# A two-layer decoder in one kernel: five small moves in the order of work

## The chip, the cores and the metric

The kernel runs on one core of a Trainium2 chip as a single launch. The metric is the device time of an execution in microseconds (us). Three runs of the kernel before give 2009.89, 2010.07 and 2011.51 us, so its time is 2010.07 us, the median. One more execution was recorded by the hardware profiler; it took 2007.35 us, and all rows below are from it.

The engines are TensorE (PE in the profile; its weight loads are PEld), VectorE (DVE), ScalarE (ACT), GpSimd (POOL) and SyncE (SP). In this kernel SP issues all plain DMAs, and POOL issues the indirect ones. Each engine carries out its instructions in order, and a DMA that has to wait on SP holds up whatever stands behind it on SP.

## What is computed

The reference is a decoder with two layers over 8 sequences of 112 tokens (896 tokens of width 512, float32), with a context of 8 x 375 rows. Each of the six parts reads a layer norm of the running sum and is added to it:

```python
x = x + L0_attn(layernorm(x), ...)                    # causal attention, 16 heads
x = x + L0_xattn(layernorm(x), ctx_2048, mask, ...)   # attention to the context
x = x + L0_ffn(layernorm(x), ...)                     # attention, then 32 experts, 8 a token
x = x + L1_attn(layernorm(x), ...)                    # causal attention, 32 heads, a bias
x = x + L1_xattn(layernorm(x), ctx_2048, mask, ...)   # attention to the context, gated
x = x + L1_ffn(layernorm(x), ...)                     # silu(x @ wg) * (x @ wu) @ wd
```

The masks of the two cross-attentions mark context rows that count or don't. For the inputs at hand only the last 96 rows of a context (`TAIL`) differ from their neighbours in the mask; all rows before (`EARLY`, 279) are masked. The kernel counts on the chip whether this holds, and has a general path if it doesn't.

## The kernel before

The tokens are seven tiles of 128 rows, `x[0]` to `x[6]`, held in SBUF; `hT` is the normalised and transposed copy (feature on the partitions) that matmuls read. The parts run one after the other, but a scheduler lays each engine's instructions out ahead of time, and it lets work of one part run beside the end of the one before where its data and memory allow it. Inside `with in_order():` the instructions of DVE, ACT, POOL and PE keep the order of the source (`Engine.issue_next`); DMAs are not pinned by it.

**Memory and waits.** A `phase` opens two pools of SBUF tiles. With `waits="pool"` the first use of a new tile waits until the whole of an older pool on the same addresses is done with; with `"tile"` it waits only for the old tiles under it. `normed_rows()` hands out a ring of three row tiles `xn`; each use waits until the third use before it is over, its store to DRAM among it. `load_w` takes one of six buffers of 1 MB (`wp`) in the same way.

**Mask counts.** `any_early()` loads both masks, counts on DVE, POOL and PE the early rows that are not masked, and leaves two numbers, `early0` and `early1`. It is called ahead of `l0_self_attention()`. Each cross-attention reads its number into a register of every engine (`by_early`) and branches to `from_last_keys` (the path taken here) or `from_all_keys`.

**First cross-attention** (`l0_cross_attention`). Its `from_last_keys` runs over the 8 sequences: scores, exponentials, the values of the sequence (`values(b)`), the turn of the outputs of the sequence before the last, the averages of the last one, and, from b = 3 on, output products and the next norm for the first `LATE` = 4 tiles (`go_on`). Behind the loop come the last turn, the last average, the end of the fourth tile and one more turn.

**Keys and values for the second cross-attention.** They depend on the context alone, so they are made earlier and kept in DRAM: `last_keys` makes the keys (`far_keys`), `last_values(b, cT, wv)` the values of one sequence (`far_values`): four matmuls, a copy by ACT into a row of the `xn` ring, and a store issued by SP. The values are made at the start of the experts (`l0_block_experts`): five sequences in the loop that normalises and transposes the tiles for the router, three in the stage that works out which token goes to which expert (`names_of`), as filling for PE. Their contexts are loaded into `wbuf[3]`, a buffer for expert weights that is not yet in use. The keys are made behind the last expert block.

**End of the experts.** The experts add their results into two DRAM arrays, `accs[0]` and `accs[1]`. Behind `last_keys` the seven `x[t]` are loaded from the first, then seven `odd[:, t]` from the second, and DVE adds them. The next layer's norms and projections follow.

**Second cross-attention and last feed-forward.** `l1_cross_attention` has a pinned loop over b = 0 to 8; in it the output products of the tiles 0 to 4 update `x[t]`; tiles 5 and 6 follow behind the branch. Then `l1_feed_forward` normalises all seven tiles (`layernorm_T`: statistics on DVE, square root on ACT, reciprocal and scaling on DVE, transposes on PE, a copy by ACT). Its matmuls use a scheme with seven products for eight, which needs sums of the two token halves of `hT` (`column_sums`, DVE, `tok`) and sums of weight blocks (`row_sums`, POOL, `sums`). `rsqrt_newton` gives the same root as `rsqrt`, by 14 small operations on POOL instead of ACT.

Most of the loops record their instructions under one line of the source, L80 (a pinned instruction), so the rows of the profile are told apart by the names of their tiles.

## Time and profile before

| what | us |
|---|---|
| median of three runs | 2010.07 |
| profiled execution, whole | 2007.35 |
| its span, first to last instruction | 2005.6 |
| PE / DVE / POOL / ACT busy | 1893.5 / 965.0 / 907.9 / 689.6 |
| mean granted TensorE clock (1 is full) | 0.975 |
| first attention | 0 to 160 |
| first cross-attention, its loop | 160 to 324, 212 to 311 |
| attention of the first layer's block | 324 to 872 |
| router and naming | 872 to 964 |
| expert blocks | 964 to 1350 |
| keys for the second cross-attention, reload of the tiles | 1350 to 1377 |
| second attention | 1377 to 1610 |
| second cross-attention | 1610 to 1741 |
| last feed-forward | 1741 to 2005 |

Times of stages are places in the profiled span. A row of the timeline gives start, length, engine, line, operation, output and input tiles with shapes, and a count where equal instructions are merged; in brackets stands how long the engine was idle before it and what ended the wait. The table of stages gives, for stretches of the span, the busy time of each engine, the granted clock, the share of the 16 DMA engines in use and the rate. The profile's digits per fortieth of the span are tenths.

### The profile page before, as it was taken

The page shows a single profiled execution, that of the slowest core. Times are in us where ns is not written, and L with a number is a line of the kernel's source. Part 1 is how long each engine was busy: PE and PEld are TensorE (multiplying, and loading weights), DVE is VectorE, ACT ScalarE, POOL GpSimd, SP SyncE. Part 2 cuts the span into 40 slices and gives each one's busy share as a digit, 9 for nine tenths or more (in the row PEclk, how much of TensorE's full clock was granted, in tenths as well). Part 3 has the DMA queues.
Part 4 walks back from the last instruction along what each step waited for, and adds up shares of the span by engine and source line. Part 5 has one row for each costly group of instructions (what it writes and reads, how often), then busy time and mean ns, then how long its engine had stood idle before and what let it go on. Part 6 is the DMA issues. An engine that isn't in the chain of part 4 may idle for free. (4 is left out here: it accounts for less than half of the span.)

```text
span 2005.6 us, 28210 instructions
## 1 busy us (share of the span) xinstructions
PE 1893.5 (94%) x10345; PEld 1233.2 (61%) x10345; DVE 965.0 (48%) x1993; ACT 689.6 (34%) x1941; POOL 907.9 (45%) x1099
## 2 busy tenths in 40 slices
PE   8999999999999999989999999998888798799999
PEld 4555565456666666754778888874456554455568
DVE  4562466486676676525222222214579656612160
ACT  3543321044444444532111111112368645432200
POOL 2253042256766765631466666640355312344371
PEclk9999988999999999989999999999999899999999
DMA  4105010233444444644986777754000020211100
GB/s 180 43 22 165 24 58 28 72 129 138 163 138 161 142 147 152 209 155 163 307 251 126 191 176 168 190 82 158 1 23 2 33 72 11 86 42 42 42 8 29
DMA packets 87469, 217.05 MB, mean 108 GB/s; under 512 B 33427, under 2 KB 41363, under 8 KB 78228
## 3 DMA queue, kind: packets, MB, share of 16 engines
q1 hardware_dynamic: 63028, 141.61, 21.0%
q0 software_dynamic: 24288, 73.47, 14.3%
q8 instruction: 87, 1.43, 0.3%
q14 instruction: 66, 0.54, 0.1%
HBM read 248.98 MB, written 82.43 MB: 165 GB/s over the span
## 5 line engine op out<-in xcount | busy, mean ns | idle before, releaser
L80 PEld LDWEIGHTS bank<-hbT,wb 128*128 128x128 f32 x1408 | 164.5, 192 | 20.5 <-issue 20.1
L80 DVE TENSOR_TENSOR hidb<-sgb,bank 128x256 f32<-128x256 f32 x66 | 27.8, 421 | 287.0 <-ACT sgb L80 213.8
L80 PE MATMUL bank<-hbT,wb 128*128 128x128 f32 x1408 | 165.0, 276 | 0.0
L1089 ACT ACTIVATE s<-s,mn 112x112 f32<-112x112 f32 x256 | 97.5, 382 | 125.1 <-DVE mn L1083 114.4
L80 POOL TENSOR_TENSOR st<-st,rec 112x448 f32<-112x448 f32 (+1 forms) x95 | 82.8, 903 | 123.4 <-DVE rec L80 77.4
L932 POOL TENSOR_TENSOR qT<-qT,qs 128x448 f32<-128x448 f32 x64 | 77.7, 1214 | 108.0 <-DVE qs L928 108.0
L80 POOL DMA_INDIRECT acc<-ob,row_out x66 | 106.3, 1610 | 35.0 <-issue 18.3
L80 ACT ACTIVATE st<-st,mxs 112x112 f32<-112x112 f32 (+1 forms) x383 | 110.9, 377 | 0.0
L80 ACT ACTIVATE sgb<-bank 128x256 f32<-128x256 f32 x66 | 25.3, 383 | 204.9 <-PE bank L80 169.6
L80 POOL DMA_INDIRECT hrow<-hrows,row_in x66 | 63.7, 965 | 54.9 <-DMA a_wo<-in_a_wo 27.3
L1096 POOL TENSOR_TENSOR s<-s,rec 112x448 f32<-112x448 f32 x64 | 64.2, 1004 | 50.2 <-DVE rec L1095 47.5
L80 POOL DMA_INDIRECT wb<-weights,wrow x44 | 46.3, 1053 | 80.8 <-PE bank L80 63.4
L80 PE MATMUL bank<-wb,hidb 128*128 128x512 f32 x176 | 82.8, 593 | 0.0
L80 ACT ACTIVATE ob<-bank,pw 128x512 f32<-128x512 f32 x66 | 45.4, 688 | 108.8 <-PE bank L80 108.8
L843 PE MATMUL bank<-tok,sums 128*128 128x448 f32 x192 | 78.1, 541 | 1.9 <-DVE tok L827 1.4
L843 PE MATMUL bank<-osum,osums 128*128 128x256 f32 x288 | 74.9, 386 | 1.4 <-POOL osums L820 1.0
L1072 PEld LDWEIGHTS bank<-kT,qT 128*112 128x112 f32 x512 | 61.6, 178 | 21.5 <-DVE s L1078 9.2
L80 PE MATMUL bank<-ident,st 112*112 112x112 f32 (+1 forms) x384 | 52.4, 271 | 21.5 <-POOL st L80 16.8
L1072 PE MATMUL bank<-kT,qT 128*112 128x112 f32 x512 | 63.1, 263 | 6.1 <-DVE s L1078 6.1
L1047 POOL TENSOR_TENSOR y<-y,oc 128x256 f32<-128x256 f32 x63 | 51.2, 817 | 38.7 <-DVE y L1045 28.7
L843 PEld LDWEIGHTS bank<-osum,osums 128*128 128x128 f32 x288 | 53.1, 192 | 24.3 <-issue 14.6
L928 DVE TENSOR_TENSOR qs<-xn,shape_consts 64x448 f32<-64x448 f32 x84 | 66.9, 797 | 1.5
(450 smaller groups left out, 4352.1 us busy)
## 6 DMA issues: line engine op xcount, KB each, us to landing
weights<-in_e_wg SPq DMA_DIRECT2D x64, 256.0 KB
weights<-in_e_wu SPq DMA_DIRECT2D x64, 256.0 KB
weights<-in_e_wd SPq DMA_DIRECT2D x64, 256.0 KB
f_wq<-in_f_wq SPq DMA_DIRECT2D x8, 1024.0 KB
f_wo<-in_f_wo SPq DMA_DIRECT2D x8, 1024.0 KB
cTe<-in_ctxT SPq DMA_DIRECT2D x8, 558.0 KB
f_wg<-in_f_wg SPq DMA_DIRECT2D x4, 1024.0 KB
f_wu<-in_f_wu SPq DMA_DIRECT2D x4, 1024.0 KB
```

Source lines behind the costliest of these rows:

```text
L80: done = issue(*args, **kw)
L843: T.matmul(dst, lhs(k), rhs(k), start=first and k == 0, stop=k == terms - 1, skip_group_check=True)
L928: V.tensor_tensor(qs[lo : lo + 64], src[hi : hi + 64], sin0[lo : lo + 64].unsqueeze(1).to_broadcast([64, HB, S]), ALU.mult,)
L932: G.tensor_tensor(d, d, qs, ALU.add)
L1047: G.tensor_tensor(d, d, more, ALU.add)
L1072: T.matmul(bank[5][:S, j * S : (j + 1) * S], qT[:, j, tok], keys[hg // 2 % 2][:, tok], start=True, stop=True)
L1089: A.activation(s[:, j, :], s[:, j, :], AF.Exp, bias=mn[:, j : j + 1], scale=-1.0, accum_out=den[:, j : j + 1])
L1096: G.tensor_tensor(s, s, rec.unsqueeze(2).to_broadcast([S, 4, S]), ALU.mult)
```

## The change

It has five parts. (1) `any_early()` is called behind `l0_self_attention()` instead of ahead of it. (2) The reload of the token tiles goes in pairs: `x[t]`, then `odd[:, t]`. (3) The values of the sequences 0 to 4 (`FAR` = 5) for the second cross-attention are made in the first: three in the rounds b = 5, 6, 7 of its loop, two behind the last average; their contexts are already there (`cTt`), and the weights `c1_wv` are loaded once more, as a fifth matrix at the start of that part. At the experts' start the sequences 5 to 7 are made in the loop over tiles, and none in the naming stage. (4) The stores of `last_keys` and `last_values` are issued by ACT. (5) The last norm goes in steps: in the second cross-attention, one round behind the update of a tile, `find_scale` works out its scale (with the root on POOL), and another round later the first three tiles are scaled into the rows of the `xn` ring; the last feed-forward takes these and does the rest of the norm for the other four. Its phase and its two inner pools wait by tile instead of by pool. The functions `last_contexts`, `last_keys` and `last_values` move up in the source.

```diff
     def last_keys(contexts, wk_):
...
-                nc.sync.dma_start(far_keys[:, c, bs, :].rearrange("p b k -> p (b k)"),
-                                  kT[:, : HB * TAIL])
+                nc.scalar.dma_start(far_keys[:, c, bs, :].rearrange("p b k -> p (b k)"),
+                                    kT[:, : HB * TAIL])
     def last_values(b, cT, wv):
...
-        nc.sync.dma_start(far_values[:, b, :], va[:TAIL])
+        nc.scalar.dma_start(far_values[:, b, :], va[:TAIL])
...
     def l0_cross_attention(early, y):
-        wq, wk_, wv, wo = (load_w(a[n], n) for n in ("c0_wq", "c0_wk", "c0_wv", "c0_wo"))
+        wq, wk_, wv, wo, c1_wv = (
+            load_w(a[n], n) for n in ("c0_wq", "c0_wk", "c0_wv", "c0_wo", "c1_wv")
+        )
...
+            def values_of_next(b):
+                return last_values(b, cTt[:, b, :, :TAIL], c1_wv)
...
                         go_on(b - 3)
+                        if b >= B - 3:
+                            all_of(values_of_next(b - B + 3))
                         waiting = b, va
                     turn_outputs(oT, *turning, tp_ps())
                     turning = average(*waiting)
+                    for b in range(3, FAR):
+                        all_of(values_of_next(b))
                     go_on(LATE - 1)
...
             for t, _ in enumerate(rmsnorm_rows_T(hT, hrows, y, ln2w)):
-                if t < 5:
-                    all_of(values_of_next(t))
+                if t < B - FAR:
+                    all_of(values_of_next(FAR + t))
...
-                far = [values_of_next(b) for b in range(5, B)]
-                next(far[0])
                 names_of(0, 2)
-                all_of(far[0])
...
                 for t in range(4, NTT):
-                    if t < 6:
-                        next(far[t - 3])
                     shared_out(t - 4)
                     names_of(t, 0)
-                    if t < 6:
-                        all_of(far[t - 3])
...
+            odd = yp.tile([P, NTT, D], FP, tag="y", name="odd")
             for t in range(NTT):
                 nc.sync.dma_start(x[t], accs[0][t * P : (t + 1) * P, :])
-            odd = yp.tile([P, NTT, D], FP, tag="y", name="odd")
-            for t in range(NTT):
                 nc.sync.dma_start(odd[:, t, :], accs[1][t * P : (t + 1) * P, :])
                 V.tensor_tensor(x[t], x[t], odd[:, t, :], ALU.add)
...
+            scales = [sm.tile([P, 4], FP, tag="mvr", name="mvr", bufs=8) for _ in range(LATE)]
+            rows = [normed_rows() for _ in range(3)]
+
+            def find_scale(t):
+                st = sm.tile([P, 6], FP, tag="bn", name="bn")
+                V.bn_stats(st, x[t])
+                V.bn_aggr(scales[t][:, :2], st)
+                rsqrt_newton(scales[t][:, 2:3], scales[t][:, 1:2], ONCE)
...
                         if b < B:
                             divide(b)
+                        if 0 <= b - 5 < len(rows):
+                            normed(rows[b - 5], x[b - 5], scales[b - 5])
+                        if 0 <= b - 4 < LATE:
+                            find_scale(b - 4)
...
-        with phase("f1") as p0:
+        with phase("f1", "tile") as p0:
             hT = new_hT()
-            layernorm_T(hT)
+            for t in range(NTT):
+                if t < len(rows):
+                    xn = rows[t]
+                else:
+                    mvr = scales[t] if t < len(scales) else row_scales(x[t])
+                    xn = normed_rows()
+                    normed(xn, x[t], mvr)
+                transpose_tile(hT, xn, t)
...
-                gp = pools.enter_context(tc.tile_pool(name="gates", bufs=1))
+                gp = pools.enter_context(tc.tile_pool(name="gates", bufs=1, reuse_waits="tile"))
...
-            with tc.tile_pool(name="down", bufs=1) as dp:
+            with tc.tile_pool(name="down", bufs=1, reuse_waits="tile") as dp:
...
-    early0, early1 = any_early()
     l0_self_attention()
+    early0, early1 = any_early()
...
-    l1_cross_attention(early1, l1_self_attention())
-    l1_feed_forward()
+    l1_feed_forward(*l1_cross_attention(early1, l1_self_attention()))
```

More of the change, by code (lines that the diff above doesn't have):

```diff
@@ L569, in tail_keys, with last_contexts, last_keys, last_values @@
                     A.activation(kT[:, c, bs, :], src, AF.Identity, bias=bias[:, c : c + 1])
+    far_keys = tc.dram_tile([P, KC, B, TAIL], FP, name="far_keys")
+    far_values = tc.dram_tile([TAIL, B, D], FP, name="far_values")
+    FAR = 5
+    def last_contexts(pool, half):
+        cT = pool.tile([P, HB, KC, TAIL], FP, tag=f"cTk{half}", name=f"cTk{half}")
+        for i in range(HB):
+            nc.sync.dma_start(cT[:, i], a["ctxT"][half * HB + i][:, :, EARLY:])
+        return cT
+    def last_keys(contexts, wk_):
+        for half, cT in enumerate(contexts):
+            bs = slice(half * HB, (half + 1) * HB)
+            for c in range(KC):
+                pp = mm_ps()
+                matmul_k(pp[:, : HB * TAIL], lambda k: wk_[:, k, c * P : (c + 1) * P],
+                         lambda k: cT[:, :, k, :])
+                kT = normed_rows()
+                A.copy(kT[:, : HB * TAIL], pp[:, : HB * TAIL])
+                nc.scalar.dma_start(far_keys[:, c, bs, :].rearrange("p b k -> p (b k)"),
+                                    kT[:, : HB * TAIL])
+    def last_values(b, cT, wv):
+        pp = tp_ps()
+        matmul_k(pp[:TAIL, :], lambda k: cT[:, k, :], lambda k: wv[:, k, :])
+        yield
+        va = normed_rows()
+        A.copy(va[:TAIL], pp[:TAIL, :])
+        nc.scalar.dma_start(far_values[:, b, :], va[:TAIL])
+        yield
     def l0_cross_attention(early, y):
-        wq, wk_, wv, wo = (load_w(a[n], n) for n in ("c0_wq", "c0_wk", "c0_wv", "c0_wo"))
+        wq, wk_, wv, wo, c1_wv = (
+            load_w(a[n], n) for n in ("c0_wq", "c0_wk", "c0_wv", "c0_wo", "c1_wv")
+        )
         with phase("c0") as p0:
@@ L762, in from_all_keys @@
                         pass
+                for b in range(FAR):
+                    all_of(values_of_next(b))
             by_early(early, "c0", from_last_keys, from_all_keys)
@@ L781, in by_early @@
         work[0] = outer
-    far_keys = tc.dram_tile([P, KC, B, TAIL], FP, name="far_keys")
-    far_values = tc.dram_tile([TAIL, B, D], FP, name="far_values")
-    def last_contexts(pool, half):
-        cT = pool.tile([P, HB, KC, TAIL], FP, tag=f"cTk{half}", name=f"cTk{half}")
-        for i in range(HB):
-            nc.sync.dma_start(cT[:, i], a["ctxT"][half * HB + i][:, :, EARLY:])
-        return cT
-    def last_keys(contexts, wk_):
-        for half, cT in enumerate(contexts):
-            bs = slice(half * HB, (half + 1) * HB)
-            for c in range(KC):
-                pp = mm_ps()
-                matmul_k(pp[:, : HB * TAIL], lambda k: wk_[:, k, c * P : (c + 1) * P],
-                         lambda k: cT[:, :, k, :])
-                kT = normed_rows()
-                A.copy(kT[:, : HB * TAIL], pp[:, : HB * TAIL])
-                nc.sync.dma_start(far_keys[:, c, bs, :].rearrange("p b k -> p (b k)"),
-                                  kT[:, : HB * TAIL])
-    def last_values(b, cT, wv):
-        pp = tp_ps()
-        matmul_k(pp[:TAIL, :], lambda k: cT[:, k, :], lambda k: wv[:, k, :])
-        yield
-        va = normed_rows()
-        A.copy(va[:TAIL], pp[:TAIL, :])
-        nc.sync.dma_start(far_values[:, b, :], va[:TAIL])
-        yield
     def row_sums(dst, top, bottom, eng):
@@ L2132, in from_all_keys @@
                     all_of(project_out(t))
+                    find_scale(t)
+                    if t < len(rows):
+                        normed(rows[t], x[t], scales[t])
             by_early(early, "c1", from_last_keys, from_all_keys)
@@ L2136, in l1_cross_attention, with l1_feed_forward @@
                 all_of(project_out(t))
-    def l1_feed_forward():
-        with phase("f1") as p0:
+        return rows, scales
+    def l1_feed_forward(rows, scales):
+        with phase("f1", "tile") as p0:
             hT = new_hT()
-            layernorm_T(hT)
+            for t in range(NTT):
+                if t < len(rows):
+                    xn = rows[t]
[4 more added lines that the diff above has]
+                transpose_tile(hT, xn, t)
             h = p0.tile([P, 16, NT], FP, tag="hid", name="hid")
             with ExitStack() as pools:
-                gp = pools.enter_context(tc.tile_pool(name="gates", bufs=1))
+                gp = pools.enter_context(tc.tile_pool(name="gates", bufs=1, reuse_waits="tile"))
                 tokens = [gp.tile([P, 2, HALF], FP, tag=f"tok{i}", name=f"tok{i}") for i in range(4)]
@@ L2244, in l1_feed_forward @@
                 in_turn(two_tiles(p) for p in range(NTT // 2))
+    l0_self_attention()
     early0, early1 = any_early()
-    l0_self_attention()
     with tc.tile_pool(name="y", bufs=1) as yp:
```

## The prediction

> **What bounds the kernel.** I read the busy shares first, then the chain of waits, then the timeline and the table of stages at the four places that the diff touches.
>
> ```profile
> span 2005.6 us, 28210 instructions
> ...
> PE 1893.5 (94%) x10345; PEld 1233.2 (61%) x10345; DVE 965.0 (48%) x1993; ACT 689.6 (34%) x1941; POOL 907.9 (45%) x1099
> ...
> PE   8999999999999999989999999998888798799999
> ```
>
> TensorE is busy 94% of the span and no other engine over half, so time can only come out of PE's gaps, or out of PE work that moves into a gap. The digits below 9 are at the start, at slice 18 (start of the experts) and in slices 27 to 34 (end of the experts to the last feed-forward). Every edit but one lies at such a place; the exception, the end of the first cross-attention, reads as a 9, so work put there has to be paid.
>
> The profiled execution took 2007.35 us: the span and 1.75 around it. The three runs have a median of 2010.07, 2.72 more. I sum against the profiled execution and take the same difference off the median.
>
> **Stores on ACT's queue, tiles reloaded in pairs (end of the experts).** The timeline there (start, length, engine, line, what; in brackets the idle time before and what ended it):
>
> ```profile
> 1358.39 0.38 SPq L803 DMA_DIRECT2D far_keys<-xn  x1
> ...
> 1363.72 0.48 ACT L80 COPY xn<-bank 128x384 f32<-128x384 f32 x1 [4.96 <-DMA far_keys<-xn]
> ...
> 1366.12 0.69 DVE L1674 TENSOR_TENSOR x<-x,odd 128x512 f32<-128x512 f32 x1 [20.49 <-DMA odd<-acc]
> ...
> 1369.58 7.12 PE L80 MATMUL bank<-cTk,c_wk 128*128 128x384 f32 x16 [2.47 <-ACT xn L80]
> ```
>
> The eight key products are 64 matmul records of 0.32 us: started at 1350.27 they could end at 1371.0; they end at 1376.7. The reader sees why: their results go through a ring of three xn rows, and the stores that free the ring stand in SP's order among 14 tile loads. The first result is ready at 1353.6, and its store is issued at 1358.39. PE loses 0.84 and 2.47 us idle and some 2 us to the lower clock that follows (0.78 in 1371 to 1377). From the last key product to the first projected chunk (1376.53 to 1390.05) PE is nearly full, so what the keys end earlier, the next layer starts earlier, if its inputs are there. With x[0], odd[0], x[1], odd[1] in turn the fourth tile is loaded after 8 transfers, not 11; I put its sum at 1367 to 1369 against 1370.3. That is in time only for an end of the keys at 1371; the score biases, now issued before 1366, should land by 1372. Next late: the bias rows and the third xn row, some 1 us. Gain 5.7 - 1 = **5**, between 3 and 6.5.
>
> No row here shows a DMA issued by ACT. The nearest is SP's 0.32 to 0.38 us for the same store. ACT has gaps of 2.1 us between the copies, so nothing waits for it; bounds 0 and 8 x 0.4 = 3 us, I take 0. Here a rule speaks against the edit: the Trainium skill (DMA: Bandwidth & Descriptors, "Issuing engines are not separate DMA queues") says that DMAs from different engines end on the same 16 DMA engines, and another issuer saves the issue time alone. The DMA share was 0.98 in 1364 to 1371, so by the rule the gain is five interleaved issues, 2 us at most. But the row shows the first store waiting 4.8 us before it is issued, in 1350 to 1364, where the share is 0.68. I take the row's 5.
>
> **Last norm in steps.** PE's timeline behind the branch that ends the last cross-attention:
>
> ```profile
> 1736.91 1.12 PE L235 MATMUL bank<-ident,xn 128*128 128x128 f32 x8
> 1740.50 0.65 PE L235 MATMUL bank<-ident,xn 128*128 128x128 f32 x4 [2.46 <-ACT hT L239]
> ...
> 1750.94 1.77 PE L843 MATMUL bank<-tok,sums 128*128 128x448 f32 x4 [1.41 <-DVE tok L827]
> 1753.08 1.02 PE L843 MATMUL bank<-tok,sums 128*128 128x448 f32 x2 [0.37 <-DVE tok L828]
> ```
>
> From 1753.08 on PE is full to the end. Between 1727.81 and there it does two output products (16 x 0.43), 7 tile transposes (7 x 0.44) and 16 records of 0.376: 6.9 + 3.1 + 6.0 = 16.0 us in 25.3; 9.3 are waits and half clock. All wait for the norm of seven tiles, one after the other on DVE and ACT, then for six sums over the token halves at 1.06 us each, slowed by POOL's weight sums beside them (0.61 alone). After the change three tiles come normalised, two with their scales, and POOL's sums, which waited 20 us for the old pool, may run early. Tile 6 still waits for its own output product: 1735 + 1.4 (residual) + 2.5 (norm) + 1 (transpose) puts the last hT tile at 1740.3 instead of 1746.8, and six sums at 0.63 end at 1744.1. PE's own work with the first product still at low clock (+1.75) ends at 1745.6; PE is the later. Gain 25.3 - 18 = **7**, between 4 and 9.
>
> What it adds: per tile 0.69 + 0.18 on DVE, 14 POOL operations at 0.27 us apart (3.8 us), and 0.55 for three rows. DVE has 3.49 us a round waiting for PE's scores, POOL 10 us; both hide it. In the last rounds the scales can push POOL's division by 0.4 us. Without that cover it is 1.4 us a round.
>
> **Five batches of c1 values.** A batch is 8 records, 3.67 us by the row of that form in the first cross-attention; five are 18.3. The timeline at both places:
>
> ```profile
> 300.36 6.05 PE L80 MATMUL bank<-vat,pTt 97*112 97x33 f32 x32
> 308.20 1.11 PE L80 MATMUL bank<-ident,xn 128*128 128x128 f32 x4 [1.79 <-DVE xn L80]
> ...
> 879.50 6.64 PE L259 MATMUL bank<-c_wv,wb 128*96 128x512 f32 x8 [2.42 <-DMA wb<-in_ctxT]
> ...
> 897.03 0.49 DVE L1242 TENSOR_SCALAR xn<-y,rms 128x512 f32<-128x512 f32 x1 [4.54 <-DMA far_values<-xn]
> ```
>
> Added in the first cross-attention: three batches in the rounds 5 to 7, 11.0 less the one gap they fill (1.12 before the last-but-one output turn), two in the tail, 7.3 less the 1.79 above, and some 3 us of slow clock that dense work can lift. The rule (TensorE: Matmul & The Clock Gate, "HAM oscillation") lets the clock fall only after gaps over about 3.4 us. The row disagrees: the longest gap before 300 is 1.12, and 300 to 312 is granted 0.50. By the rule a batch costs 3.67 and the sum is 12; by the row it may cost up to 6.6, as at 879.50, and the sum is 30. Of the 64 value records in that very stage the median is 0.592, the shortest; so I take the full rate. Cost **12**, bounds 8 and 30.
>
> Removed at the experts' start: two of five batches in the loop over tiles, 7.2, and the 1.56 us PE waited there for the xn row (its store behind SP's loads): 9 at the router. DVE's routing (about 11 us) follows and shifts with it. Of the three batches in the naming stage PE would wait anyway for 2.1 us in the first (one-hots) and all of the second; 4.5 gained. The value weights are free earlier, so the 1 MB a_wo load of 950.6 leaves the place where the first expert rows are fetched and the stores of the shared outputs wait (PE idle 2.58 before 964.26): 1.5. Gain **15**, bounds 7 and 18. Net **-3**.
>
> Also moved: the loads of the value weights take a slot of the weight ring; the next six loads move one slot later. f_wk goes from 144 to about 160, the first query weights to about 274, needed at 324: covered.
>
> **Mask counts later.** At the start DVE's 1.29 and 2.46 us and one PE operation leave; PE's first projection at 15.12 waited for a transpose behind them: 0.5. Behind the first layer the two small loads can start only when its memory is released (160), and the counts take about 3 + 5 us, to 169. The first query copy (166.48) reuses that memory, but PE has the other bank until 171.8; DVE is idle 163.8 to 167.6. What hangs on it is SP: eight context loads at 160.28 with the chain of one-buffer loads behind, which ends 0.7 us before PE's scores at 212.34. Bounds -1.5 and +8; taken +1.5 - 0.5 = **+1**.
>
> **Sum**: -5 - 7 - 3 + 1 = -14: a profiled execution near 1993.4, a median of **1996**.
>
> **Rivals.** (a) *The experts' start does not follow* (0.20): the values were cover for DVE's routing and for transfers. For it: 1.04 DMA share in 872 to 880, and two of three late batches hidden. Against: PE is full in 896 to 913. Gain 6 instead of 15: 2005. (b) *More comes back* (0.15): the half-rate stretches in 300 to 324 and after 1728 go with their gaps, and the token tiles never wait: experts -18, tail +8, norm -9, keys -6: about 1986. (c) *Slower: the clock at the end of the first cross-attention* (0.10). If the five batches run at half rate, 33 us, less 3 for gaps, and the sums near them stay slow, the net is +30 - 15 = +15 and +3 for the neighbours; with -11 from the rest: 2017. It decides once that stage grows by more than 30 us. For it: 0.50 in 300 to 312; against: the median of 0.592.
>
> **Chances.** Main case 0.55, its own range 1989 to 2003. A measurement of this kernel tells about 0.2% (4 us) from no change. Main case all but a little, half of (a) and all of (b) are below 2006: faster 0.78; same 0.11; slower, (c) and the mask counts at their bad end, 0.11. The range that leaves out no more than 2 in 10 runs from 1983 to 2009.
>
> **What would show it.** In the new profile: key stores 0.5 us behind each copy and the keys' last product near 1371 less the shift; full PE from about 18 us after the branch at the last layer instead of 28; 40 value records of 0.59 in the first cross-attention, 24 later; the router 9 us nearer to the last query head. Wrong: those records at 1.1, the first context loads later than 165, or an unchanged distance from the router to the first expert.

## The result

The change makes the kernel slower. The medians of four runs each are 2025.62 us after and 2009.98 us before, a ratio of 1.0076 (95% interval 1.0058 to 1.0094), some 15 us where 14 less were forecast. The profiled execution took 2021.77 us, 14.4 more than that of before. One thing has to be known for what follows: single runs of one kernel spread widely, those of before from 2002 to 2018 us over 43 runs, so that parts of 2 us are told apart only by many runs, and a stage of one trace is certain to some 3 us: the stretch from the first average to the first query took 102.6 to 105.9 us in seven kernels whose code is the same up to there.

### The profile page after: what moved, and what is told of

Its sections match the earlier page's. It is cut to its first block, busy times and chain, and to the rows that moved or that the text cites. A ratio compares the mean times of both kernels' runs of the same rounds, so it can differ in the third digit from the quotient of the medians.

```text
span 2020.0 us, 28261 instructions
## 1 busy us (share of the span) xinstructions
PE 1891.6 (94%) x10345; PEld 1228.0 (61%) x10345; DVE 969.0 (48%) x1988; ACT 688.8 (34%) x1936; POOL 920.1 (46%) x1169
## 4 chain that ended last, share of the span: by engine, by line
PE 54%; DVE 11%; POOL 9%; issue 8%; DMA 4%; ACT 2%; SPq 1%; POOLq 0%; DVEq 0%; ACTq 0%
PE bank L857 23%; PE bank L80 17%; PE bank L259 8%; POOL acc L80 3%; PE bank L1086 2%; POOL hrow L80 2%; PE bank L1121 2%; DMA acc<-ob,row_out 2%; DVE mxs L80 2%; DVE den L80 1%; DVE qs L942 1%; POOL st L80 1%; SPq L581 1%; PE bank L1077 1%; PE bank L1114 1%
## 5 line engine op out<-in xcount | busy, mean ns | idle before, releaser
L80 PEld LDWEIGHTS bank<-hbT,wb 128*128 128x128 f32 x1408 | 164.8, 193 | 20.8 <-issue 20.7
L857 PEld LDWEIGHTS bank<-osum,osums 128*128 128x128 f32 x288 | 53.1, 192 | 24.0 <-issue 14.4
```

The lines of the kernel that those rows point to most:

```text
L80: done = issue(*args, **kw)
L857: T.matmul(dst, lhs(k), rhs(k), start=first and k == 0, stop=k == terms - 1, skip_group_check=True)
```

## The profile after

The page first: span, busy shares and the digits of PE.

```profile
span 2020.0 us, 28261 instructions
...
PE 1891.6 (94%) x10345; PEld 1228.0 (61%) x10345; DVE 969.0 (48%) x1988; ACT 688.8 (34%) x1936; POOL 920.1 (46%) x1169
...
PE   8999998999999999987999999998888798799999
```

PE's busy time is what it was (1893.5 before), as it must be: the five batches have only moved. The span grew by 14.4, so PE's idle time grew from 112 to 128 us. Two digits have changed: the seventh, 303 to 353 us, where the first cross-attention ends (9 before, 8 now), and the nineteenth, 909 to 960 us, where the routing and naming are (9 before, 7 now). By these digits no gap that the change was to fill has become smaller, and two places are worse.

Landmarks of PE's timeline show where. The shift is the start of the first row of its kind after, less that before:

| landmark on PE | before | after | shift | step and its forecast |
|---|---|---|---|---|
| first context key (`cTt,c_wk`) | 191.51 | 188.47 | -3.0 | mask counts, +1 |
| first average (`vat,pTt`) | 221.36 | 221.37 | 0.0 | the same |
| first query of the next part (`hT,f_wq`) | 323.94 | 337.02 | +13.1 | five batches, +12 |
| its second half (`x,f_wq`) | 416.27 | 431.98 | +15.7 | not forecast |
| sixth expert block (`hbT,wbh`) | 993.82 | 1004.94 | +11.1 | experts' start, -15 |
| first key (`cTk,c_wk`) | 1350.27 | 1364.24 | +14.0 | expert loop, 0 |
| first value of the next layer (`a_wv,hT`) | 1429.93 | 1447.00 | +17.1 | keys and tiles, -5 |
| end of the last branch (`pTt,vat`) | 1725.19 | 1742.07 | +16.9 | 0 |
| first `tok,f_wg`, PE full | 1757.84 | 1771.99 | +14.2 | last norm, -7 |

The steps are the differences between one shift and the next: 13.1, 2.6, -4.6, 2.9, 3.1, -0.2 and -2.7 make the 14.2 of the last row. The large misses are the experts' start (-4.6 for -15) and the keys (+3.1 for -5). The +2.9 of the expert loop is at the edge of what one trace can tell, and its cause was not looked for.

At the experts' start, the rows of the DMA queue, DVE and PE in the router loop are these, after the change and then before it:

```profile
909.56 0.33 SPq L157 DMA_DIRECT2D a_wv<-in_a_wv  x1
...
909.99 8.01 SPq L1257 DMA_DIRECT2D hrows<-xn  x3
...
917.16 0.49 DVE L1256 TENSOR_SCALAR xn<-y,rms 128x512 f32<-128x512 f32 x1 [5.02 <-DMA hrows<-xn]
...
929.96 0.18 PE L80 MATMUL bank<-ones,earlier 128*32 128x1 bf16 x1 [3.35 <-DVE earlier L80]
```

```profile
918.59 0.18 PE L80 MATMUL bank<-ones,earlier 128*32 128x1 bf16 x1 [1.09 <-DVE earlier L80]
...
941.26 0.35 SPq L157 DMA_DIRECT2D a_wv<-in_a_wv  x1
```

The last batch of values ends on PE at 909.54. That sets the buffer of the value weights free, and 0.02 us later SP starts the load that needs a buffer next, the 1 MB `a_wv`. SP had stood in front of this load for 5.8 us. The stores of normalised rows (`hrows<-xn`) behind it are late: the row of the fourth tile was ready at 907.23, and its store is issued at 909.99. Then they share the DMA engines with the load (0.79 of them in use in 911 to 916). The ring of rows comes free late, and DVE waits 5.02 us before it can norm the sixth tile; the third of the stores merged over 8.01 us is that tile's own, at 917.67. PE waits 2.55 us for the tile, and the routing that follows the last tile comes late. There PE waits 3.35 us, where it was 1.09 before: of the 12 filling products that stand in this wait before the change, 6 stand earlier now. Before the change this load started at 941.26, behind the router.

In the expert blocks a second wait appears. The rows are a gather of weights (1.5 MB), the gather of the fifth block's token rows, and PE, and then PE's row for the fifth block before the change:

```profile
972.22 0.99 POOL L80 DMA_INDIRECT wbh<-weights,wrow  x1 [0.30 <-issue]
...
977.06 0.96 POOL L80 DMA_INDIRECT hrow<-hrows,row_in  x1 [3.85 <-issue]
...
988.50 1.11 PE L80 MATMUL bank<-ident,hrow 128*128 128x128 f32 x4 [3.49 <-DMA hrow<-hrows,row_in]
```

```profile
980.21 0.60 PE L80 MATMUL bank<-ident,hrow 128*128 128x128 f32 x4
```

The row block that is issued behind three gathers of weights is there for PE only 11 us later. Before, PE reached this place after it was there.

The keys, on ACT and PE:

```profile
1367.10 0.48 ACT L77 COPY xn<-bank 128x384 f32<-128x384 f32 x1 [4.67 <-PE bank L80]
...
1367.61 0.36 ACTq L593 DMA_DIRECT2D far_keys<-xn  x1
...
1375.71 0.29 ACT L191 ACTIVATE mvr<-mvr,eps 128x1 f32<-128x1 f32 x1 [6.43 <-DVE mvr L223]
...
1375.92 0.46 ACT L80 COPY xn<-bank 128x384 f32<-128x384 f32 x1
...
1376.43 14.86 PE L80 MATMUL bank<-cTk,c_wk 128*128 128x384 f32 x40 [4.21 <-ACT xn L80]
```

The first tile's sum starts on DVE at 1374.0, 9.8 us behind the first key product, where it took 15.9 before: the pairs do what they are meant to. But the square root of that tile's norm (`mvr`) now stands on ACT ahead of the second key copy. ACT, which goes in order, waits 6.43 us for the tile, and PE waits 4.21 for the copy.

## Experiments

Each kernel ran beside the kernel before on the same chip; ratios are to that, with their 95% intervals, and 0.001 is 2 us.

### The five batches

**Values alone**: the kernel before with part (3) of the change, all stores on SP.

> The kernel before with the values of the sequences 0 to 4 moved, and nothing else (stores still on SP). Theory from the two traces: first cross-attention +13 (18.3 of new products less about 3 of filled gaps, less 2 of clock), the next norm +2.6 behind it, the experts' start gives back 5 instead of 15, because the transfers that the first expert blocks need can't start earlier by the same amount: net +9 to +13 us against before, and PE waits some 3.5 us for a gathered row between the third and the fourth expert block. Rival, the sum of the forecast: the experts' start gives back 15, net -3. Rival, the loss of the whole change is elsewhere (the pairs, the waits by tile): within 3 us of before, and no wait for a gathered row.

2022.59 us, ratio 1.0062 (1.0039 to 1.0084), some 12 us of loss, as the theory has it, and PE waits 3.51 us for the gathered row block. The move of the values is most of the loss.

**Values, weights held**: the same, and one small product that still reads the value weights behind the router.

```diff
                 fill(4)
                 product()
+                T.matmul(tp_ps()[:1, :1], c1_wv[:, 0, :1], c1_wv[:, 0, :1])
                 names_of(0, 2)
```

> Values alone with one thing more: a 1 x 1 product that reads the value weights stands in the naming stage, so that their buffer comes free, and the next layer's value weights (1 MB) are loaded, some 20 us later. Theory: that load, which moved from 941 to 910 us when the values left, is what holds up the row stores of the router loop (DVE waits 5 us there for a row store); held back, the router's first sigmoid stands 3 to 5 us nearer to the loop's first router product, and the time is 2 to 5 us below values alone: 2018 to 2021. Rival: the load is in the way wherever it stands, the gain at the router is lost again until the fifth expert block: within 1.5 us of values alone. Rival: the wait there has nothing to do with the load, no change in the router loop.

2015.37 us, ratio 1.0030 (1.0019 to 1.0040): some 6 us less than values alone, for a product of 0.2 us; the two intervals just touch. `a_wv` is loaded at 935.03, DVE has no wait for a row store left in the loop (4.29 us in values alone), and PE waits 1.09 us for routing, not 3.46. The scheduler also keeps 12 filling products for that wait, where it kept 4, so the load itself and the order that was laid out around it are not told apart.

**Contexts later**: values alone, and the loads of the contexts for the keys held back to the ninth block.

```diff
+                    if i == 8:
+                        for half in range(2):
+                            V.memset(tiles[half][:1, :, 0, :1], 0.0)
+                            for j in range(HB):
+                                nc.sync.dma_start(tiles[half][:, j],
+                                                  a["ctxT"][half * HB + j][:, :, EARLY:])
```

> Values alone with the eight loads of contexts for the keys (1.5 MB) held back until the ninth expert block by a small write into their tiles. Theory: the first expert blocks wait for transfers; with these loads away the fifth gathered row block comes in time, PE's wait of 3 to 4 us between the third and fourth block goes, and the sixth block starts 4 to 6 us earlier relative to the first one: 3 to 6 us below values alone. Rival: the gather waits for its turn on POOL or for the stores of the shared outputs, the wait stays as it is: within 1.5 us of values alone.

2026.92 us, ratio 1.0087 (1.0074 to 1.0101), and the wait for the row block is 4.78. The expectation was wrong. But the experiment was not clean: the load of `c_wg` (1 MB) then came 29 us earlier, into the same place, so that what these loads cost the row block stays open.

**Rows first**: values with held weights, and the fifth row block gathered ahead of the weights of the blocks 4 and 5.

```diff
-                for i in range(3, NWB - 1):
-                    load_weights(i)
+                load_weights(3)
...
+                    if i == 0:
+                        load_rows(i + NROWS)
+                        load_weights(NWB - 2)
```

> Values alone with the weights held, and one thing more: the fifth gathered row block is issued ahead of the weights of the expert blocks 4 and 5 (each 1.5 MB) instead of behind. Theory: the row block waits behind three gathers of weights in the DMA queues; ahead of two of them it comes in time, PE's wait of 3.5 us between the third and the fourth block goes, unless the weights come late instead: -2 to -4 us against values held (2015.4). Rival: the row block waits for the stores of the shared outputs, issued before it: the wait stays, no change within 1.5 us. Rival: the weights of block 4 come late by as much: the wait moves there, no change or up to +3.

2015.11 us, ratio 1.0023 (1.0011 to 1.0035), where held weights alone had 1.0030: nothing that can be told from no gain. PE's rows for the fifth and the sixth block show why:

```profile
981.17 0.60 PE L80 MATMUL bank<-ident,hrow 128*128 128x128 f32 x4
...
989.49 0.66 PE L80 MATMUL bank<-ident,hrow 128*128 128x128 f32 x4 [2.43 <-DMA hrow<-hrows,row_in]
```

The fifth block's wait (3.53 us with the weights held) is gone, as the theory says. But the sixth row block now stands behind three gathers of weights, and PE waits 2.43 us for that one. The wait has moved on by a block.

**Two batches**: only two sequences moved, both behind the last average, with their stores on ACT; three stay in the router loop and three in the naming stage.

```diff
-    FAR = 5
+    FAR = 2
...
-                        if b >= B - 3:
-                            all_of(values_of_next(b - B + 3))
...
-                    for b in range(3, FAR):
+                    for b in range(FAR):
...
-                if t < B - FAR:
+                if t < 3:
```

> The kernel before with only the values of the sequences 0 and 1 moved, both behind the last average of the first cross-attention (ACT stores these two, SP the others); three stay in the router loop and three in the naming stage, as before. Theory: a batch costs its 3.7 us of PE where PE has no gap and nothing where it had one, so two batches in the tail, which had gaps of 1.1, 1.8 and 1.6, cost 4 to 6 with what the next norm loses; the router loop gives back two batches, 6 to 9, and the naming batches keep the value weights in use: -1 to -5 us against before. Rival: what the first cross-attention loses is not PE time but the later weight loads and the order on DVE behind it, the same for two batches as for five: cost 8 or more, +1 to +4.

2011.49 us, ratio 1.0003 (0.9988 to 1.0018). From the first average to the first query it grew by 7.7 us for 7.3 us of products: in sum the gaps there were not filled, 1.12, 1.79 and 1.55 before and 1.10, 0.24 and 3.91 now. The next norm took 2.6 more, and from `x,f_wq` to the sixth expert block it got back 7.6. Between 2 us of gain and 4 of loss nothing is told; neither the theory nor the rival is settled.

### The keys and the token tiles

**Pairs alone**, and **the changed kernel with the old reload** (the same edit the other way round):

```diff
+            odd = yp.tile([P, NTT, D], FP, tag="y", name="odd")
             for t in range(NTT):
                 nc.sync.dma_start(x[t], accs[0][t * P : (t + 1) * P, :])
-            odd = yp.tile([P, NTT, D], FP, tag="y", name="odd")
-            for t in range(NTT):
                 nc.sync.dma_start(odd[:, t, :], accs[1][t * P : (t + 1) * P, :])
```

> The kernel before with the token tiles reloaded in pairs, and nothing else (key stores still on SP). Theory: with the first tile expected earlier, the square root of its norm comes to stand on ACT ahead of the second key copy, and ACT, which goes in order, waits there for the tile: the second key copy comes 7 us or more behind the first, PE idles 4 us or more in the key products, and the time is 2 to 5 us above before. Rival: the order of the roots doesn't matter, since the x tiles come 11 us earlier in pairs; the pairs bring the first tile's sum forward and the time is 1 to 3 us below before. Rival: transfers set this stage either way, no change within 1 us.

> The changed kernel with the reload as it was before (seven x, then seven odd), stores still on ACT's queue. Theory: the roots stand behind the fourth key copy again, the key products run through, and the stage from the first key product to the first projection chunk is 4 to 8 us shorter than in the changed kernel: 2018 to 2022. Rival: the tiles are late by the DMA load and not by the pairs, within 2 us of the changed kernel.

Pairs alone: 2010.61 us, ratio 0.9998 (0.9987 to 1.0009). PE waits 3.46 us for the second copy, nearly as long as the theory says, but the stage to the next layer's first value is 80.0 us long, and was 79.7: the wait costs nothing that shows. The old reload: 2026.95 us, ratio 1.0081 (1.0058 to 1.0103), no better than with pairs, and that stage 82.8 as in the changed kernel. So the pairs aren't the loss, and both theories were wrong on the time. The stores on ACT's queue came under suspicion. ACT's rows of the latter kernel show them:

```profile
1373.21 0.48 ACT L80 COPY xn<-bank 128x384 f32<-128x384 f32 x1 [2.10 <-PE bank L80]
...
1378.63 0.34 ACTq L593 DMA_DIRECT2D far_keys<-xn  x1
...
1379.07 0.48 ACT L80 COPY xn<-bank 128x384 f32<-128x384 f32 x1 [5.38 <-DMA x<-acc]
```

The second key copy ends at 1373.69. Its store is issued at 1378.63, 4.9 us later, and the third copy stands behind it. The store's row doesn't say what it waited for; the profile names a load of `x` as what ends ACT's idle time, so an earlier DMA is the likely cause, and that isn't shown.

**Stores on ACT alone**:

```diff
-        nc.sync.dma_start(far_values[:, b, :], va[:TAIL])
+        nc.scalar.dma_start(far_values[:, b, :], va[:TAIL])
...
-                nc.sync.dma_start(far_keys[:, c, bs, :].rearrange("p b k -> p (b k)"),
+                nc.scalar.dma_start(far_keys[:, c, bs, :].rearrange("p b k -> p (b k)"),
```

> The kernel before with the stores of keys and values issued by ACT, and nothing else. Theory, from the changed kernel with the old reload (second key store issued 4.9 us behind its copy, ACT idle, third copy late): a store that ACT issues also waits in ACT's order[...], so the copies behind it come late, and the stage from the first key product to the first value product of the next layer grows by 2 to 4 us (79.7 before): +2 to +4 us. Rival, the forecast's mechanism: SP's order was what held the stores, the ring comes free earlier, -3 to -5 us. Rival: the pairs made the loss, so stores on ACT alone are within 1 us of before.

2009.68 us, ratio 0.9995 (0.9982 to 1.0008), that is -3.6 to +1.6 us. The stage is 84.6 us long, 4.9 more than before, but the time of the whole doesn't show it: the theory's +2 to +4 lies outside the interval, the rival "within 1 us" inside it, and of the forecast's gain (-3 to -5) only the smallest value.

**Key stores on POOL**, which has nothing else to do there:

```diff
-                nc.sync.dma_start(far_keys[:, c, bs, :].rearrange("p b k -> p (b k)"),
+                nc.gpsimd.dma_start(far_keys[:, c, bs, :].rearrange("p b k -> p (b k)"),
```

> The kernel before with the eight key stores issued by POOL, which has nothing to do there, and nothing else. Theory: what undid the gain from ACT's stores is that their waits stand in ACT's order among the key copies; on POOL they hold nobody up, the ring is free in time, PE's two waits for the xn rows go, and the stage from the first key product to the first value product of the next layer is 2 to 5 us shorter than before's 79.7; time -2 to -5. Rival: the transfers set the stage (DMA share 0.98 there), the tiles are late and the stage is as long as before within 1 us.

2014.28 us, ratio 1.0021 (1.0009 to 1.0034). The theory was wrong, and the stage is 85.5 us long. Four copies go at the pace of the products, with no wait for the ring, and then ACT does this:

```profile
1363.43 0.48 ACT L80 COPY xn<-bank 128x384 f32<-128x384 f32 x1 [2.15 <-PE bank L80]
...
1370.71 0.29 ACT L191 ACTIVATE mvr<-mvr,eps 128x1 f32<-128x1 f32 x1 [5.50 <-DVE mvr L223]
...
1370.91 0.46 ACT L80 COPY xn<-bank 128x384 f32<-128x384 f32 x1
```

The fifth copy stands behind the first root, and the root waits for the tile.

**Keys first**: the stores on POOL, and the norm of the next layer pinned behind the keys, so that all eight copies go ahead of the roots.

```diff
             hT = new_hT()
-            layernorm_T(hT)
+            with in_order():
+                layernorm_T(hT)
```

> The kernel before with the key stores issued by POOL, and the next layer's norm pinned behind the keys, so that all eight key copies stand on ACT ahead of the first square root. Theory: with POOL's stores the fifth copy still waited for the first root (ACT idle 5.5 us), and that, not the stores, is what holds the key products; with the roots behind, the eight key products run through in 21 us instead of 26.4, and the first value product of the next layer comes 2 to 5 us earlier than before's 79.7 after the first key product: -2 to -5 us. Rival: the norms then begin late, since the last three stores hold the ring of rows, and what the keys gain the next layer's start loses: keys 21 us, but the distance to the first value product within 1 us of 79.7 or longer.

2020.40 us, ratio 1.0046 (1.0030 to 1.0062): 9 us slower than before. PE's rows:

```profile
1355.17 21.49 PE L80 MATMUL bank<-cTk,c_wk 128*128 128x384 f32 x62
...
1378.85 3.50 PE L1707 MATMUL bank<-rows,flip 112*112 112x448 f32 x8 [2.19 <-DMA rows<-in_a_bias]
...
1394.06 3.35 PE L259 MATMUL bank<-hT,a_wq 128*128 128x448 f32 x4 [0.68 <-ACT hT L80]
```

The rival holds. The keys run through in 22.6 us where before took 26.4, but the norms then begin late, the first projection chunk starts 40 us behind the first key product (33 before), and the stage is 86.7 us long. So a norm that comes later makes the stage longer, however early the keys end. The run doesn't show that shorter keys alone buy nothing: the pin also takes the tiles of the norm one by one (DVE starts the second tile's statistics at 1382.92, when the first is scaled), where before the scheduler had them overlap. With the stores on ACT, on POOL and with the keys first the stage is longer each time (84.6, 85.5 and 86.7 us); a run with short keys and an undisturbed norm was not made.

### Mask counts and last norm, alone

```diff
-    early0, early1 = any_early()
     l0_self_attention()
+    early0, early1 = any_early()
```

> The kernel before with the mask counts called behind the first layer, and nothing else. Theory, from the changed kernel's trace: the first context keys come 3 us earlier, because the queries are no longer held up at their second tile, but the second sequence's scores then wait for DVE (1.4 us idle and 1.6 of half clock), and from the third on the loop stands where it stood: 0 within 1 us, keys 2 to 3 us earlier. Rival, the forecast: +1, keys later than before. Rival: the 3 us are kept, -3.

2010.40 us, ratio 1.0011 (1.0000 to 1.0022): at most 4 us of loss, and no gain. The first keys come 3.6 us earlier and the first average 1.4. Two rows of the changed kernel show what stops it, DVE's last sum over a context and PE's second group of scores:

```profile
211.97 1.32 DVE L643 TENSOR_REDUCE cTt<-cTe 128x4 f32<-128x1116 f32 x1 [4.24 <-SPq L820]
...
215.33 2.59 PE L80 MATMUL bank<-qT,kTt 32*96 32x112 f32 x32 [1.41 <-DVE pTt L77]
```

The sums over contexts hang on loads that share one buffer, one after another. Their last ends at 213.3 here and at 211.3 before; the mask terms and the clamp of the first scores (`pTt`) follow on DVE. PE is there earlier and waits. The group then takes 2.59 us, not 1.02; the expectation put that down to half clock, but the granted clock is 1.00 in 214 to 218. PE's quarters of the group start at 215.33, 215.87, 216.40 and 216.93, each some 0.06 us behind the end of one of DVE's four clamps, so it goes at DVE's pace.

**The norm in steps** (part 5 of the change, with its waits by tile):

> The kernel before with the last norm in steps and the waits by tile in the last feed-forward, and nothing else. Theory: the stage is bound by the chain of tiles 5 and 6 behind the second output product, which the change doesn't shorten; the loop of the second cross-attention grows by 1 and the last stage shrinks by 3: -1 to -3 us. Rival, the forecast: -7 us. Rival: POOL's root steps in the last rounds delay its division, the loop grows as much as the last stage shrinks: 0 within 1 us.

2007.85 us, ratio 0.9990 (0.9978 to 1.0002): in the theory's range, and just not told from no gain. From the last branch's end to full PE it takes 29.7 us, 32.7 before, and the loop of the second cross-attention grows by 1.7.

### Mending the changed kernel

**The changed kernel with the weights held**, by the same product as above:

> The changed kernel with the 1 x 1 product that keeps the value weights in use, so that the next layer's value weights are loaded after the router loop. Theory: in the full change too the router loop is held up by that load (DVE waits 5 us for a row store); with it held back the time falls by 4 to 8 us to 2017 to 2021. Rival: with the value stores on ACT's queue the row stores have another cause of waiting: within 2 us of the changed kernel.

2015.99 us, ratio 1.0025 (1.0014 to 1.0036), 10 us below the changed kernel, more than the theory's 4 to 8. SP and DVE now read:

```profile
913.59 2.00 SPq L1257 DMA_DIRECT2D hrows<-xn  x2
...
932.82 0.35 SPq L157 DMA_DIRECT2D a_wv<-in_a_wv  x1
...
914.37 0.87 DVE L1256 TENSOR_SCALAR xn<-y,rms 128x512 f32<-128x512 f32 x1 [0.81 <-DMA far_values<-xn]
```

The row stores go out at once, the load follows at 932.82, DVE's wait is 0.81, and PE waits 1.10 us for routing. From `x,f_wq` to the sixth expert block it takes 561.4 us, where the changed kernel took 573.0 and before 577.6.

On top of that, the **key stores on SP and the old reload**, then the **mask counts at the start**, then the **rows first**; and, from the kernel before, the **norm in steps with the keys first**:

> The changed kernel with the value weights held, the key stores issued by SP again and the reload in its old order; the value stores stay with ACT. Theory: what remains of the loss after the weights are held (5.4 us) is partly the waits that the key stores brought into ACT's order (83 to 84 us from the first key product to the first value product where SP's stores have 79.7): 2 to 4 us below the changed kernel with held weights: 2012 to 2014. Rival: the stage with SP's stores is no shorter when the rest of the change is there: within 1.5 us of 2016.

> The kernel of the run with held weights and SP's key stores, with the mask counts at the start again. Theory: the counts alone cost 1 to 2 us (1.0011 in their own run), as the loop of the first cross-attention gives back the 3 us that the keys came earlier: 1 to 2 us below that kernel. Rival: the counts' effect at the start (0.6 us) is all there is: within 1 us, or above.

> The changed kernel with held weights, SP's key stores, the old reload and the mask counts at the start (2009.8), and the fifth gathered row block issued ahead of the weights of the blocks 4 and 5. Theory: what is left to gain at the experts' start is PE's wait for that row block, 1.6 us there: 2006 to 2009, 1 to 4 us below before. Rival: the expert loop gives it back, within 1.5 us of 2009.8.

> The kernel before with the last norm in steps, the key stores on POOL and the norm pinned behind the keys; nothing moved into the first cross-attention. Theory: the two gains add, -2 from the last norm and -2 to -5 from the keys: 2003 to 2007, below both kernels. Rival: the keys' part gives nothing, then it is at the time of the last norm alone, 2008.

| kernel | median us | ratio to before | interval |
|---|---|---|---|
| changed | 2025.62 | 1.0076 | 1.0058 to 1.0094 |
| weights held | 2015.99 | 1.0025 | 1.0014 to 1.0036 |
| and key stores on SP, old reload | 2013.90 | 1.0013 | 1.0003 to 1.0022 |
| and counts at the start | 2009.78 | 0.9996 | 0.9982 to 1.0009 |
| and rows first | 2011.39 | 0.9993 | 0.9979 to 1.0007 |
| before, norm in steps, keys first | 2016.57 | 1.0027 | 1.0014 to 1.0040 |

The differences of the first ratios are 10, 2.4 and 3.4 us. Key stores on SP and the old reload meet their theory (2012 to 2014), but the first difference alone stands clear of the intervals; those of the other two steps overlap, and only their sum, 5.8, stands clear. In the traces the first average comes at 225.54 with the counts behind the first layer and at 221.57 with them at the start, which is 4 us, more than the expectation had. What is left, the five batches with their stores on ACT and their weights held, and the norm in steps, is at the time of before.

With the rows first the wait again moves to the sixth block (1.60 us, after 1.63 at the fifth), and nothing is gained: the rival holds. The norm in steps with the keys first missed both its theory (2003 to 2007) and its rival (2008); its stage from the keys on is 86.0 us long, as with the keys first alone. No kernel here is below before by more than its interval; nearest is the norm in steps alone.

## Why the prediction was wrong

Between the forecast (-14) and the trace (+14.2) lie 28 us: 10.4 at the experts' start, 8.1 at the keys, 4.3 at the last norm, 2.9 in the expert loop, 2.6 in the norm behind the five batches and 1.1 in the batches, less some 1 elsewhere.

**Five batches, what they give back.** This is the step that failed: "The value weights are free earlier, so the 1 MB a_wo load of 950.6 leaves the place where the first expert rows are fetched". A buffer that comes free is taken by whatever load is next. Before the change `a_wv` took the buffer of the shared expert's weights (`wgus`, whose last product ends at 941.23) and `a_wo` that of the value weights (950.57). Now the value weights are the first to come free, so `a_wv` took theirs, among the row stores of the router loop at 909.56, and `a_wo` waits for the other, until 953.39. With the buffer held, the experts' start gains 16.1 us in the changed kernel and 13.0 in values alone, so the forecast's 15 was about the right size of what the removal can give. Without that, it gains 4.6 and 6.5: the early load took 11.6 and 6.5 us away again (2.6 of the 11.6 lie in the attention ahead of the router, within what one trace can tell).

Rival (a) named the place and a transfer as the cause, and put the gain at 6; it was 4.6. It named cover for DVE as well. The 3.35 us in which PE waits for routing are not that, since they are 1.10 with the weights held and no batch there either. Cover that is missing shows in the naming stage: PE waits 1.41 and 2.99 us there for ACT (`athigh`), waits that before doesn't have.

**Five batches, what they cost.** 13.1 for 12: right, and the batches do run at the full rate but for one. PE's row ahead of the last output products before the change, then PE's rows behind the loop after it, and DVE's at the next norm:

```profile
311.61 12.49 PE L259 MATMUL bank<-c_wo,oT 128*128 128x512 f32 x24 [1.55 <-ACT oT L80]
```

```profile
305.52 4.95 PE L80 MATMUL bank<-c_wv,cTt 128*96 128x512 f32 x8
...
313.76 7.09 PE L80 MATMUL bank<-c_wv,cTt 128*96 128x512 f32 x16
...
324.93 12.26 PE L259 MATMUL bank<-c_wo,oT 128*128 128x512 f32 x24 [2.80 <-issue]
...
331.14 0.69 DVE L221 BATCH_NORM_STATS2 bn<-d 128x6 f32<-128x512 f32 x1
...
333.79 0.75 DVE L656 SCALAR_TENSOR_TENSOR d<-bank,rs,bo 128x512 f32<-128x512 f32 x1 [1.95 <-PE bank L259]
...
334.46 0.17 DVE L223 BATCH_NORM_AGGREGATE mvr<-bn 128x2 f32<-128x6 f32 x1
```

One batch of eight takes 4.95 us, two together 7.09. Dense work did lift the slow clock: the granted clock in 300 to 312 is 0.86, not 0.50, and the last average takes 3.24 us, not 6.05. The gaps of 1.12 and 1.79 us were filled, but the wait ahead of the last output products is now 2.80 (1.55 before). Rival (c), half clock for more than 30 us, did not come about. Missing in the sum is the next norm, +2.6 here and +6.1 in values alone. The weights came in time here (`f_wk` at 170, the query weights at 279, for 160 and 274 forecast), but on DVE the residual of the second tile now stands ahead of the aggregate of the first, which could start at 331.8 and starts at 334.46; that the order costs the 2.6 is read from the rows and wasn't tried. One part of the change helps here: in the seven traces in which ACT issues the stores of the moved values, the stretch from the first query to `x,f_wq` is 94.9 to 95.0 us long, in the four in which SP does it is 97.2 to 98.4. Why was not followed.

**Keys, stores, pairs.** -5 was forecast from "what the keys end earlier, the next layer starts earlier, if its inputs are there", and "ACT has gaps of 2.1 us between the copies, so nothing waits for it". Both failed. In the changed kernel the keys end no earlier, as a root stands in front of their second copy: they take 27.1 us, 26.4 before, and 20.7 were forecast. And the forecast followed the inputs of the next layer to the sum of the fourth tile, not to the norm of all seven: the run with the keys first shows 3.8 us won by the keys and 10.8 lost behind them, as its norm came later. Whether keys that end early would gain anything with the norm in time stays open. The second sentence failed because the gaps of ACT are no cover for an instruction that waits: everything behind it waits with it, 6.43 us for a tile in the changed kernel and 4.9 at a store in the run with the old reload. The rule of the Trainium skill (DMA: Bandwidth & Descriptors, "Issuing engines are not separate DMA queues") that was weighed there against the row, that another issuer saves issue time alone, gave 2 at most; the row gave 5. No gain was measured, so the rule was nearer than the row, which told why a store was late but not what its being early was worth.

**Mask counts.** +1 forecast, 0.0 at the first average in the trace, and 0 to 4 by the runs: the forecast lies inside. The chain of one-buffer loads behind which the forecast saw 0.7 us of slack is indeed what ends last there, so the 3 us that the queries gained were lost, which the forecast had not got.

**Last norm.** -7 forecast, -2.7 measured here and -3.0 alone. The mechanism is right and its last term was too small. PE, POOL and DVE:

```profile
1745.30 5.30 PE L259 MATMUL bank<-c_wo,oT 128*128 128x512 f32 x8 [3.22 <-issue]
...
1754.61 0.75 POOL L834 TENSOR_TENSOR sums<-f_wg 128x256 f32<-128x256 f32 x1 [7.09 <-PE bank L259]
...
1755.57 1.24 DVE L1982 SCALAR_TENSOR_TENSOR x<-g,x 128x512 f32<-128x512 f32 x1
...
1765.67 2.52 PE L857 MATMUL bank<-tok,sums 128*128 128x448 f32 x6 [1.39 <-DVE tok L841]
```

The two output products still come first, the first of them at 5.30 us (the granted clock is 0.70 in 1745 to 1750.6), so the second ends 12.4 us behind the branch, where the forecast had 9.8. From there to the normed row of the last tile it takes 5.5 us and not 3.9: DVE scales two other tiles in between, and its 0.69 us operation takes 1.24 beside POOL. POOL's weight sums were to come early; they still wait 7.09 us for PE's output product, also with waits by tile, and so run beside DVE's work as before. The last hT tile is ready 19.3 us behind the branch (21.6 before, 15.1 forecast), and PE then waits for the token sums.

**The odds.** 0.78 for faster came from three steps counted as likely gains, each argued from its own stage. What a step does to the transfers of another stage was followed for the buffers that the change fills, and not for those that it empties.

## What to carry to other kernels

When work is moved away, list what it was holding: the buffer that comes free is a transfer that starts, and it starts in front of whatever is queued behind it; where it hurts, a product of 0.2 us that still reads the buffer holds it back. Before paying for a shorter stage, find what the next one would wait for then: the keys gained 3.8 us in one run, and the stage grew by 7. A DMA issued by a computing engine brings its waits into that engine's order, and gaps in the engine's time don't hide them.

## What the runs showed of the hardware

- A DMA that ACT issues took 0.31 to 0.36 us of ACT's queue in the changed kernel, and one that could not go at once (old reload) held ACT for 4.9 us. Issued by POOL, the same key stores took 0.54 to 0.67.
- A gather of token rows that was issued behind three gathers of weights (1.5 MB each) was there for PE only 11 us after its issue; put ahead of two of them, it came in time, and the next one was waited for.
- In before the granted clock was 0.50 in 300 to 312, where PE's longest gap was 1.79 us; with the batches in these gaps it was 0.86.
- Another order of the loads gave another order of the instructions: with the tiles in pairs the scheduler put the first root ahead of the second key copy, and ACT waited 6.4 us for the tile.
- The 43 runs of before spread over 15 us (2002.38 to 2017.80) at mean granted clocks of 0.972 to 0.982; the two fastest had the two highest (0.982 and 0.980), but at 0.976 alone the times go from 2005.4 to 2015.8.
